# Expert choice with its token norms taken by VectorE from the transposed rows, and the expert weights loaded between those rows

## The chip, the cores and the metric

The kernel runs on one core of a Trainium2 chip. A core has a matrix engine (TensorE, in the profile PE, with its weight loads as PEld), a vector engine (VectorE, DVE), an engine for activations and copies (ScalarE, ACT), a general one (GpSimd, POOL) and SyncE (SP), which here only issues DMAs. Operands lie in SBUF (128 partitions), TensorE writes to PSUM (eight banks of 128 x 512 float32), and sixteen DMA engines carry data between SBUF and DRAM. The metric is the time of one execution in microseconds on the device; less is better.

## The reference

The program is a four-layer network on an image of 4 x 128 x 64 x 64 in float32: 4 batches of 4096 tokens of 128 channels. Each layer is a token mixer and a feed-forward part, both with residuals. The feed-forward part of layers 1 and 2 is a mixture of 64 experts in which each expert chooses its 8 tokens in each batch. The norm ahead of it has no weights. Cut to this part:

```python
def _ln_t(v, eps=1e-5):                       # per token, over 128 channels
    m = jnp.mean(v, axis=-1, keepdims=True)
    s = jnp.var(v, axis=-1, keepdims=True)
    return (v - m) / jnp.sqrt(s + eps)

def _L1_ffn_ref(x, gate_w, gate_b, weight1, weight2):
    logits = jnp.einsum('bsd,ed->bse', x, gate_w) + gate_b
    probs = jax.nn.softmax(logits, axis=1)                     # over the 4096 tokens
    vals, idx = jax.lax.top_k(probs.transpose(0, 2, 1), K)     # 8 tokens of each expert
    topv, topi = vals.transpose(0, 2, 1), idx.transpose(0, 2, 1)
    flat_idx = topi.reshape(Bn, K * E)
    gathered = jnp.take_along_axis(x, flat_idx[:, :, None], axis=1).reshape(Bn, K, E, Dn)
    pooled = jnp.einsum('bked,bke->bed', gathered, topv)
    ...                       # h = gelu([pooled, 1] @ weight1), out = [h, 1] @ weight2
    weighted = jnp.einsum('beo,bke->bkeo', out, topv).reshape(Bn, K * E, O)
    return jnp.zeros((Bn, Sn, O)).at[jnp.arange(Bn)[:, None], flat_idx].add(weighted)

t = t + _L1_ffn_ref(_ln_t(t), ...)            # layer 1; the same in layer 2
```

The logits of a token can be had from the token as it is: with a gate matrix from which the channel mean has been taken (`cent` @ gate), they are the product times 1/sqrt(variance + eps), plus the bias. Likewise the pooled token is `cent` times the sum of raw tokens, each weighted by its share times its 1/sqrt.

## The kernel before, in words

The activations `net.xs` stay in SBUF, channels on the partitions, tokens along the free axis; `net.chunk(b, c)` is chunk c (512 tokens, eight a batch) of batch b. `expert_choice` (L1246) is called for layers 1 and 2. Batches are worked on in two pairs, batches 0 and 1 and batches 2 and 3: the 64 experts of one batch lie on partitions 0 to 63, those of the other on 64 to 127.

Each call has three stages. Stage A finds norms, logits, choices and pooled tokens. Stage B is the experts' network, 16 groups of four experts (`first`, `turn`, `second`, `hand`), each group with two weight DMAs of 1 MiB (`load`, L1320 and L1322). Four groups have buffers of their own (`moe_w`) and are loaded ahead; the fifth buffer (`moe_w_b`) takes the place of stage A's pools, so its first load waits until those are released. Stage C adds the experts' outputs to the chosen tokens (L1629, L1633).

Stage A before, by its functions:

- `load` of four groups (8 MiB) comes first in the program.
- `stat(p, j)`: centres 512 tokens with a matmul by `cent` (L1343) and squares them on ScalarE (L1345). `variances` sums four squares over the channels with matmuls by `ewin` (L1353), so that one PSUM bank gathers the variances of a pair, 512 tokens to a partition. `scales` takes the square root on ScalarE (L1366), `inverted` the reciprocal on VectorE (L1370, 128 x 512). `turn_scales` transposes the scales so that tokens lie on partitions (L1376, L1378).
- `logits(p, c)`: a matmul broadcasts a chunk's scales to the experts' partitions (L1387), two gate matmuls make the raw logits (L1389), ScalarE copies the broadcast (L1393), VectorE multiplies (L1394), ScalarE adds the bias (L1395). The result stays in `chosen[p]`, 128 x 4096.
- `rows(b, c)`: four transposes put 512 tokens on partitions (L1417), ScalarE copies them into one of five buffers `xts` (L1419) with their scale behind them (L1420), and a DMA writes them to a table in DRAM, 144 floats a token (L1422).
- `largest(p)`: VectorE finds the 8 largest of 4096 logits in each partition and their places (L1428, L1431) and turns the places into table rows (L1433 to L1437). `exponentials` and `denominators` make the softmax sums on ScalarE (L1445, L1449). `ask(p, j)` gathers rows on POOL's queue (L1455).
- `pool(p)`: for each of the 8 choices VectorE makes a diagonal of share times scale (L1469) and TensorE adds up rows times diagonal (L1477); a copy, the matmul by `cent` (L1481) and the copy to `pooled` (L1482) follow.

TensorE, ScalarE, VectorE and POOL execute in the order in which the program is written (`manual_schedule(engines=ORDERED)`); a buffer taken from a pool makes an instruction wait until the previous user is done. SP's order is made by the framework's scheduler; SP executes its DMA issues one after another, so one that waits for data holds those behind it. The attention phase, which the prediction draws on, also has a scale row that goes to DRAM and is broadcast back (`att_spread`, L1922, and `att_by`, L1927), a root taken on VectorE in 14 steps (L1855 to L1861); and the last feed-forward part takes token statistics on VectorE (L2485).

Of the kernel before, what the change touches and what calls it, by code (L numbers as in the profile page):

```python
# [17 lines left out]
F32 = mybir.dt.float32  # L18
# [1227 lines left out]
def expert_choice(net, layer):  # L1246
# [20 lines left out]
    K, ROW = 8, P + 16  # L1267
# [3 lines left out]
    with ExitStack() as ctx:  # L1271
        dram = ctx.enter_context(tc.tile_pool(name="moe_dram", bufs=1, space=bass.MemoryType.DRAM))
        tables = [dram.tile([2 * N, ROW], F32, name=f"moe_table{p}") for p in range(PAIRS)]
# [24 lines left out]
        behind = keep.tile([P, 1], F32, name="moe_behind")  # L1298
        nc.gpsimd.memset(behind[0:E], 0.0)
        nc.gpsimd.memset(behind[E:P], float(N))  # L1300
# [24 lines left out]
        weights = [load(g) for g in range(EARLY)]  # L1325
        with (
# [5 lines left out]
            def bank(tag, name):  # L1332
                return ps.tile([P, CH], F32, name=f"moe_{name}", tag=tag, bufs={"a": 3, "b": 3}.get(tag, 1))

            stats = {}

            def stat(p, j):

                if j == 0:
                    stats[p] = (bank("pv", "pv"), [])  # L1340
                pv, squares = stats[p]
                pd = bank("a", "pd")
                nc.tensor.matmul(pd, net.cent, net.chunk(2 * p + j // NCH, j % NCH), start=True, stop=True)  # L1343
                sq = sb.tile([P, CH], F32, name="moe_sq", tag="moe_sq", bufs=5)
                nc.scalar.activation(sq, pd, AF.Square)  # L1345
                squares.append(sq)
                if j % 4 == 1 and j > 4:
                    variances(p, j // 4 - 1)

            def variances(p, r):  # L1350
                pv, squares = stats[p]
                for q in range(4):
                    nc.tensor.matmul(  # L1353
                        pv[32 * q : 32 * q + 32],
                        net.ewin[:, 31 - r : 63 - r],
                        squares[4 * r + q],
                        start=r == 0,
                        stop=r == 3,
                    )

            rstds, turned = {}, {}

            def scales(p):
                variances(p, 3)
                rstd = sb.tile([P, CH], F32, name="moe_rstd", tag="moe_rstd")
                nc.scalar.activation(rstd, stats[p][0], AF.Sqrt, bias=net.eps[1e-5])  # L1366
                rstds[p] = rstd

            def inverted(p):
                nc.vector.reciprocal(rstds[p], rstds[p])  # L1370

            def turn_scales(p):

                pt = bank("a", "pr")
                for k in range(4):
                    nc.tensor.transpose(pt[:, k * P : (k + 1) * P], rstds[p][:, k * P : (k + 1) * P], net.ident)  # L1376
                turned[p] = sb.tile([P, 2, NCH, 4], F32, name="moe_turned", tag="moe_turned")
                nc.vector.tensor_copy(  # L1378
                    turned[p].rearrange("p i (a q) k -> p k q (i a)", q=4),
                    pt.rearrange("p (k q r) -> p k q r", q=4, r=32)[:, :, :, 0:4],  # L1380
                )

            def logits(p, c):
                pb, pl = bank("b", "rb"), bank("a", "pl")
                q = c % 4
                rows = slice(32 * q, 32 * q + 32)
                nc.tensor.matmul(pb, own[rows, c // 4, :], rstds[p][rows], start=True, stop=True)  # L1387
                for i in range(2):
                    nc.tensor.matmul(  # L1389
                        pl[i * E : (i + 1) * E], cgate, net.chunk(2 * p + i, c), start=True, stop=True  # L1390
                    )
                lg = chosen[p][:, c * CH : (c + 1) * CH]
                nc.scalar.copy(lg, pb)  # L1393
                nc.vector.tensor_mul(lg, lg, pl)  # L1394
                nc.scalar.activation(lg, lg, AF.Identity, bias=gbias)  # L1395

            xts = [sb.tile([P, 4, ROW], F32, name=f"moe_xt{i}", bufs=1) for i in range(5)]
            for t in xts:
                nc.gpsimd.memset(t[:, :, P:ROW], 0.0)

            own = sb.tile([P, 2, 2 * E], F32, name="moe_own", bufs=1)
            for q in range(4):
                group = slice(32 * q, 32 * q + 32)
                for r in range(2):
                    for i in range(2):
                        at = 32 * q + 2 * i + r
                        nc.gpsimd.tensor_copy(
                            own[group, r, i * E : (i + 1) * E], net.ident[group, at : at + 1].to_broadcast([32, E])
                        )

            def rows(b, c):

                p, i = divmod(b, 2)
                pt = bank("b", "pt")
                for t in range(4):
                    tok = slice((4 * c + t) * P, (4 * c + t + 1) * P)
                    nc.tensor.transpose(pt[:, t * P : (t + 1) * P], net.xs[:, b, tok], net.ident)  # L1417
                xt = xts[(b * NCH + c) % len(xts)]
                nc.scalar.copy(xt[:, :, 0:P], pt.rearrange("p (t d) -> p t d", d=P))  # L1419
                nc.scalar.copy(xt[:, :, P], turned[p][:, i, c, :])  # L1420
                first = i * N + c * CH
                nc.sync.dma_start(tables[p][first : first + CH, :].rearrange("(t p) r -> p t r", p=P), xt)  # L1422

            places, shares, asked = {}, {}, {}

            def largest(p):
                top = keep.tile([P, K], F32, name=f"moe_top{p}")
                nc.vector.max(out=top, in_=chosen[p])  # L1428
                tops[p] = top
                place = sb.tile([P, K], U32, name="moe_place", tag="moe_place")  # L1430
                nc.vector.max_index(out=place, in_max=top, in_values=chosen[p])  # L1431
                row = sb.tile([P, K], F32, name="moe_row", tag="moe_row")
                nc.vector.tensor_copy(row, place)  # L1433
                nc.vector.tensor_scalar(row, row, behind, None, op0=ALU.add)
                places[p] = sb.tile([P, K], I32, name="moe_idx", tag="moe_idx")
                nc.vector.tensor_copy(places[p], row)
                nc.vector.tensor_scalar_mul(negs[p], top[:, 0:1], -1.0)  # L1437
# [3 lines left out]
            def exponentials(p, c):  # L1441

                sq = sb.tile([P, CH], F32, name="moe_sq", tag="moe_sq", bufs=5)
# [8 lines left out]
            def ask(p, j):  # L1452
                if j == 0:
                    asked[p] = sb.tile([P, K, ROW], F32, name="moe_asked", tag="moe_asked")
# [6 lines left out]

            def pool(p):

                nc.vector.reciprocal(totals[p], totals[p])
                nc.vector.tensor_scalar_mul(shares[p], shares[p], totals[p])
                acc = bank("acc", "acc")[:, 0 : 2 * E]
# [1185 lines left out]
```

## Time and profile before

| what | us |
|---|---|
| median of the runs (3) | 6021.36 (6016.81 to 6021.89) |
| the profiled execution's own time | 6020.81 |
| its span, first to last instruction | 6018.7 |
| stage A of layer 1 | 2466.5 to 2588.0, 121.5 |
| stage B of layer 1 | 2588.0 to 2665.0, 77.0 |
| stage A of layer 2 | 2933.7 to 3053.2, 119.5 |
| stage B of layer 2 | 3053.2 to 3130.0, 76.8 |
| mean granted TensorE clock | 0.975 of full speed |

The two stages A are 241 us, 4% of the span. Their end is taken where SP issues the first late weight load. Window rows are read thus: stretch in us, its length, then for each engine busy time and (instructions), the granted TensorE clock, the mean busy share of the DMA engines (the records can overlap, so a little over 1 is possible) and GB/s. Timeline rows: start, duration, engine, line, operation, output <- inputs, shapes, how many; in square brackets the idle time of the engine before it and what ended it. For SP (`SPq`) the duration is that of the issue, not of the transfer. Rows of waits: engine and line, what was waited for, us in total, times, the longest.

### The profile page before, as it was taken

How to read it: one execution, taken by the hardware profiler on the slowest of the kernel's cores; microseconds unless marked ns; L12 is line 12 of the kernel's file. 1: busy time of each engine (PE TensorE's matmuls, PEld its weight loads, DVE VectorE, ACT ScalarE, POOL GpSimd, SP SyncE). 2: the span in 40 equal slices, each digit the busy share in tenths (PEclk: the TensorE clock that was granted, in tenths of full speed). 3: DMA queues.
4: the chain of work that ended last, by engine and by line, in shares of the span. 5: the costliest groups of instructions: out<-in, count | busy, mean ns of one | idle time of the engine just before them, and what ended most of it. 6: DMA issues, size and time to landing. Idle time of an engine off the chain costs nothing. (4 is left out here: it accounts for less than half of the span.)

```text
span 6018.7 us, 97982 instructions
## 1 busy us (share of the span) xinstructions
PE 5660.1 (94%) x39902; PEld 2247.3 (37%) x39933; DVE 4413.8 (73%) x4945; ACT 3332.5 (55%) x4150; POOL 2057.3 (34%) x2015
## 2 busy tenths in 40 slices
PE   8999999889999988879979999999999999999699
PEld 2222222346677666433333222322232223222243
DVE  6888887456667676357446888888888888888687
ACT  4444444332333232431336888888888888899410
POOL 3898897027777777200010111111111111111100
PEclk9999999999999999989989999999999999999899
DMA  6434432047777777550274676656665666666300
GB/s 216 99 73 92 86 78 47 1 142 222 220 231 216 231 220 211 163 203 0 81 266 112 131 158 146 140 127 151 146 144 125 150 146 144 130 136 133 69 25 28
DMA packets 273275, 818.40 MB, mean 136 GB/s; under 512 B 42644, under 2 KB 100392, under 8 KB 226728
## 3 DMA queue, kind: packets, MB, share of 16 engines
q0 software_dynamic: 109568, 505.75, 35.4%
q1 hardware_dynamic: 163240, 306.20, 17.6%
q8 instruction: 320, 5.24, 0.4%
q14 instruction: 147, 1.20, 0.1%
HBM read 416.71 MB, written 93.13 MB: 85 GB/s over the span
## 5 line engine op out<-in xcount | busy, mean ns | idle before, releaser
L2035 ACT ACTIVATE att_ex<-att_sc,att_shift 128x1024 f32<-128x1024 f32 x2048 | 2141.7, 1111 | 282.6 <-PE att_sc L2031 167.7
L2066 DVE TENSOR_TENSOR att_dve<-att_dve,att_ex 128x2048 f32<-128x2048 f32 x704 | 1631.5, 2317 | 155.3 <-ACT att_ex L2035 130.5
L2031 PE MATMUL att_sc<-att_q,att_k 32*128 32x512 f32 x8192 | 1280.9, 640 | 0.5 <-ACT att_ex L2035 0.5
L2047 PE MATMUL att_pv<-att_ex,att_vals 128*32 128x512 f32 x8192 | 1091.9, 605 | 0.0
L998 POOL DMA_INDIRECT dcn_g<-dcn_table,dcn_idx x896 | 851.4, 950 | 354.2 <-issue 151.1
L412 DVE SCALAR_TENSOR_TENSOR inv_prod<-inv_pk,bspan,inv_seen 128x512 f32<-128x512 f32 (+1 forms) x1120 | 774.6, 743 | 140.1 <-PE inv_pk L399 139.8
L410 POOL TENSOR_TENSOR inv_prod<-inv_seen,inv_prod 128x512 f32<-128x512 f32 (+1 forms) x672 | 837.5, 1273 | 94.0 <-ACT inv_prod L409 94.0
L2064 POOL DMA_DIRECT2D att_dma<-att_ex x224 | 192.5, 860 | 1965.4 <-ACT att_ex L2035 1727.4
L409 ACT ACTIVATE inv_prod<-inv_pk,bspan 128x512 f32<-128x512 f32 (+1 forms) x672 | 436.1, 682 | 503.7 <-PE inv_pk L399 493.9
L2031 PEld LDWEIGHTS att_sc<-att_q,att_k 32*128 32x128 f32 x8192 | 423.0, 183 | 658.4 <-issue 417.1
L1006 DVE TENSOR_TENSOR dcn_g<-dcn_g,dcn_near_w 128x1024 f32<-128x1024 f32 x448 | 539.0, 1214 | 167.9 <-DMA dcn_g<-dcn_table,dcn_idx 151.7
L399 PE MATMUL inv_pk<-inv_red,wtap 32*96 32x512 f32 (+1 forms) x3584 | 511.4, 636 | 7.3 <-DVE wtap L377 7.3
L1015 PE MATMUL dcn_pt<-ident,dcn_g 128*128 128x128 f32 x3584 | 473.1, 276 | 37.5 <-ACT dcn_st L1120 12.6
L1015 PEld LDWEIGHTS dcn_pt<-ident,dcn_g 128*128 128x128 f32 x3584 | 418.9, 142 | 210.1 <-issue 122.7
L421 PE MATMUL inv_out<-inv_prod,inv_fold 96*32 96x512 f32 (+1 forms) x3584 | 477.9, 605 | 8.5 <-DVE xs L429 8.5
L2047 PEld LDWEIGHTS att_pv<-att_ex,att_vals 128*32 128x32 f32 x8192 | 161.2, 108 | 752.6 <-issue 727.4
L399 PEld LDWEIGHTS inv_pk<-inv_red,wtap 32*96 32x96 f32 (+1 forms) x3584 | 131.5, 170 | 385.6 <-DVE inv_prod L412 362.1
L1120 ACT COPY dcn_st<-dcn_pt 128x512 f32<-128x512 f32 x224 | 129.9, 580 | 241.2 <-PE dcn_pt L1015 241.2
L1034 ACT ACTIVATE dcn_fold<-dcn_pf,dcn_turn 128x256 f32<-128x256 f32 x128 | 60.2, 473 | 365.1 <-PE dcn_pf L1030 365.1
L1127 PE MATMUL dcn_out<-dcn_st,dcn_wk 128*128 128x512 f32 x448 | 237.4, 612 | 23.3 <-DVE xs L1135 21.4
L2554 PE MATMUL top_po<-top_xg,top_cwe 128*128 128x512 f32 x512 | 233.7, 597 | 0.0
L1054 DVE TENSOR_TENSOR dcn_square<-dcn_hx,dcn_by 128x512 f32<-128x512 f32 x192 | 130.1, 678 | 114.2 <-PE dcn_by L1040 75.2
(449 smaller groups left out, 5326.1 us busy)
## 6 DMA issues: line engine op xcount, KB each, us to landing
att_dma<-att_ex POOLq DMA_DIRECT2D x224, 1024.0 KB, 7.0
inv_seen<-inv_image SPq DMA_DIRECT2D x256, 266.0 KB, 9.1
moe_w<-in_L_ffn_weight SPq DMA_DIRECT2D x64, 1024.0 KB, 14.4
att_dma<-att_ex SPq DMA_DIRECT2D x32, 1024.0 KB, 11.2
att_dve<-att_dma POOLq DMA_DIRECT2D x32, 1024.0 KB
moe_table<-moe_xt SPq DMA_DIRECT2D x64, 288.0 KB, 2.8
dcn_table<-dcn_xt SPq DMA_DIRECT2D x32, 512.0 KB, 4.8
dcn_g<-dcn_table,dcn_idx POOLq DMA_INDIRECT x896, 3.7
```

Of the source, the lines that this page charges most:

```text
L399: nc.tensor.matmul(pk[0:m], wtap[half][rg, i, blk], red[rg, h * CH : (h + 1) * CH], start=True, stop=True)
L409: nc.scalar.activation(prod[0:m, h], pk[0:m], AF.Identity, bias=by)
L410: nc.gpsimd.tensor_mul(of, view, of)
L412: nc.vector.scalar_tensor_tensor(out=of, in0=as_shape(pk[0:m], of), scalar=by, in1=view, op0=ALU.add, op1=ALU.mult)
L421: nc.tensor.matmul(po[CR * blk : CR * (blk + 1), h, :], fold[0:m], prod[0:m, h, :], start=unit == 0, stop=unit == UNITS - 1,)
L998: nc.gpsimd.indirect_dma_start(out=g[:, t, :], out_offset=None, in_=rows, in_offset=bass.IndirectOffsetOnAxis(ap=idx[:, Q4 * c + i + t, k ...
L1006: nc.vector.tensor_mul(near, near, by)
L1015: nc.tensor.matmul(pt[0][:, (i + t) * P : (i + t + 1) * P], near[:, t, q, :], net.ident, is_transpose=True, start=i + t + q == 0, stop=i + ...
L2031: nc.tensor.matmul(pes[h // 2][:, h % 2, :], ks[r, t * P : (t + 1) * P], q[r], start=True, stop=True)
L2035: nc.scalar.activation(ex[:, 2 * two : 2 * two + 2, :], pes[two], AF.Exp, bias=shifts[g][:, two : two + 1],)
L2047: nc.tensor.matmul(block["pv"][r], vals[:, t, r], ex[:, h, :], start=t == 0, stop=t == NT - 1)
L2066: nc.vector.tensor_add(block[who], block[who], ex)
```

## The change

- Statistics: `rows(b, c)` now also makes them. The four transposes take every fourth token of a chunk (so that each partition holds four neighbouring tokens and the table is written in runs of 2 KB), and VectorE's `bn_stats` reads each 128 x 128 block from PSUM. `stat`, the `ewin` matmuls and `turn_scales` go. The table has 128 floats a token, without the scale.
- Scales: `scales(p)` makes variances (`variance`, five small steps), root, reciprocal (now 128 x 64) and one transpose; a row of scales goes to DRAM (`spread`) and comes back broadcast to the experts' partitions, chunk by chunk (`way`, two DMAs of 128 KB, three buffers `moe_by`), in place of the broadcast matmul.
- Logits: the multiply reads the broadcast and the product in the strided order in which the rows lie.
- Choice: `largest_of` finds the 8 largest of each chunk as it comes; `largest` finds the 8 largest among the 64 candidates and their table rows, with tables `behind` and `order` filled by POOL one column at a time.
- Pooling: the scale of the gathered rows is computed from the gathered rows themselves (`bn_stats`, `variance`, `inverse_root`) ahead of the diagonals.
- Order: rows of batches 0 and 1 first; the weight loads stand behind every second row of batch 1 instead of at the start; then the scales of pair 0, the centring of the gate, six rows of batch 2, and the logits of pair 0 with the remaining rows and the scales of pair 1 between them; the second pair's logits go along with the first pair's gathers and exponentials.

In the built program's order on SP, layer 2's loads stand behind 10, 12, 14 and 16 row writes; in layer 1 the first load stays ahead of the rows and the other three stand behind 12, 14 and 16. In both, the first `spread` row and the broadcasts `way` stand behind the last load.

```diff
-    K, ROW = 8, P + 16
+    K, HALVES = 8, 6
...
-        tables = [dram.tile([2 * N, ROW], F32, name=f"moe_table{p}") for p in range(PAIRS)]
+        tables = [dram.tile([2 * N, P], F32, name=f"moe_table{p}") for p in range(PAIRS)]
+        spread = [dram.tile([2, NCH, CH], F32, name=f"moe_spread{p}") for p in range(PAIRS)]
...
+        behind = keep.tile([P, NCH, K], F32, name="moe_behind")
+        for c in range(NCH):
+            nc.gpsimd.memset(behind[0:E, c, :], float(c * CH))
+            nc.gpsimd.memset(behind[E:P, c, :], float(N + c * CH))
+        order = keep.tile([P, NCH * K], F32, name="moe_order")
+        for i in range(NCH * K):
+            nc.gpsimd.memset(order[:, i : i + 1], float(i))
...
-        weights = [load(g) for g in range(EARLY)]
+        weights = []
...
+            def variance(halves, out, apart):
+                nc.vector.tensor_sub(apart, halves[..., 1], halves[..., 4])
+                nc.vector.tensor_mul(apart, apart, apart)
+                nc.vector.tensor_add(out, halves[..., 2], halves[..., 5])
+                nc.vector.scalar_tensor_tensor(
+                    out=out, in0=apart, scalar=P / 4.0, in1=out, op0=ALU.mult, op1=ALU.add
+                )
+                nc.vector.tensor_scalar(out, out, 1.0 / P, 1e-5, op0=ALU.mult, op1=ALU.add)
...
             def rows(b, c):
...
+                    nc.tensor.transpose(pt[:, t * P : (t + 1) * P], net.chunk(b, c)[:, t:CH:4], net.ident)
                 xt = xts[(b * NCH + c) % len(xts)]
+                nc.scalar.copy(xt, pt.rearrange("p (t d) -> p t d", d=P))
+                for t in range(4):
+                    nc.vector.bn_stats(halves[p][:, i, c, t, :], pt[:, t * P : (t + 1) * P])
                 first = i * N + c * CH
+                nc.sync.dma_start(tables[p][first : first + CH, :].rearrange("(p t) r -> p t r", t=4), xt)
...
             def scales(p):
...
+                variance(halves[p].rearrange("p i c t h -> p (i c t) h"), var, apart)
+                nc.scalar.activation(var, var, AF.Sqrt)
+                nc.vector.reciprocal(var, var)
                 pt = bank("a", "pr")
+                nc.tensor.transpose(pt[0 : 2 * NCH * 4, 0:P], var, net.ident)
+                lines = sb.tile([2 * NCH * 4, P], F32, name="moe_lines", tag="moe_lines", bufs=1)
+                nc.vector.tensor_copy(lines, pt[0 : 2 * NCH * 4, 0:P])
+                nc.sync.dma_start(spread[p].rearrange("i c (t q) -> (i c t) q", q=P), lines)
+                for c in range(2):
+                    way(p, c)
+
+            def way(p, c):
+                by = ways[p, c] = sb.tile([P, CH], F32, name="moe_by", tag="moe_by", bufs=3)
+                for i in range(2):
+                    nc.sync.dma_start(by[i * E : (i + 1) * E], spread[p][i, c : c + 1, :].to_broadcast([E, CH]))
...
             def logits(p, c):
-                pb, pl = bank("b", "rb"), bank("a", "pl")
...
-                nc.scalar.copy(lg, pb)
-                nc.vector.tensor_mul(lg, lg, pl)
+                by = ways.pop((p, c)).rearrange("p (t q) -> p q t", t=4)
+                nc.vector.tensor_mul(lg.rearrange("p (q t) -> p q t", t=4), by, pl.rearrange("p (q t) -> p q t", t=4))
                 nc.scalar.activation(lg, lg, AF.Identity, bias=gbias)
+                if c + 2 < NCH:
+                    way(p, c + 2)
...
+            def largest_of(p, c):
+                lg = chosen[p][:, c * CH : (c + 1) * CH]
+                nc.vector.max(out=peaks[p][:, c, :], in_=lg)
+                nc.vector.max_index(out=spots[p][:, c, :], in_max=peaks[p][:, c, :], in_values=lg)
...
             def largest(p):
...
+                nc.vector.max(out=top, in_=flat)
+                nc.vector.tensor_scalar_mul(negs[p], top[:, 0:1], -1.0)
+                nc.vector.max_index(out=place, in_max=top, in_values=flat)
+                nc.vector.tensor_copy(at, place)
+                nc.vector.tensor_copy(known, spots[p])
+                nc.vector.tensor_add(known, known, behind)
+                for j in range(K):
+                    nc.vector.scalar_tensor_tensor(
+                        out=found[:, j, :],
+                        in0=order,
+                        scalar=at[:, j : j + 1],
+                        in1=known.rearrange("p c k -> p (c k)"),
+                        op0=ALU.is_equal,
+                        op1=ALU.mult,
+                    )
...
             def pool(p):
...
+                for j in range(K):
+                    nc.vector.bn_stats(own[:, j, :], asked[p][:, j, :])
+                var, root, spare = (small[:, n] for n in range(3))
+                variance(own, var, spare)
+                inverse_root(root, var, spare, small[:, 3].bitcast(I32))
+                nc.vector.tensor_mul(shares[p], shares[p], root)
                 for j in range(K):
...
+                    nc.vector.tensor_scalar(diag, net.ident, shares[p][:, j : j + 1], None, op0=ALU.mult)
+                    nc.tensor.matmul(acc, asked[p][:, j, :], diag, start=j == 0, stop=j == K - 1)
...
+            for b in range(2):
+                for c in range(NCH):
+                    rows(b, c)
+                    if b and c % 2:
+                        weights.append(load(len(weights)))
             scales(0)
...
+            left = [(b, c) for b in range(2, B) for c in range(NCH)]
+            for _ in range(6):
+                rows(*left.pop(0))
             for c in range(NCH):
                 logits(0, c)
+                for _ in range(2):
+                    if left:
+                        rows(*left.pop(0))
+                        if not left:
+                            scales(1)
+                if c > 0:
+                    largest_of(0, c - 1)
+            largest_of(0, NCH - 1)
             largest(0)
             for c in range(NCH):
                 logits(1, c)
+                ask(0, c)
+                exponentials(0, c)
+                if c > 0:
+                    largest_of(1, c - 1)
             denominators(0)
+            largest_of(1, NCH - 1)
             largest(1)
+            for c in range(K):
+                ask(1, c)
                 exponentials(1, c)
             denominators(1)
             pool(0)
...
             pool(1)
```

## The prediction

> **What bounds the kernel now.** I read the page's first part for the balance of engines, then the table of windows for the two passes through `expert_choice`, then the issue queue of SP (SyncE) and its waits for the moment that ends the changed part, and last the timeline of VectorE for prices. TensorE leads overall, but the diff touches only stage A of each pass (statistics, logits, choice, gather, pooling), so the window table counts:
>
> ```profile
> PE 5660.1 (94%) x39902; PEld 2247.3 (37%) x39933; DVE 4413.8 (73%) x4945; ACT 3332.5 (55%) x4150; POOL 2057.3 (34%) x2015
> ```
> ```profile
> core 0: us, PE busy (x) PEld busy (x) DVE busy (x) ACT busy (x) POOL busy (x), PEclk, DMA share, GB/s
> 2466.50:2588.00 121.50, 102.89 (x402) 44.96 (x402) 44.03 (x59) 73.70 (x168) 16.24 (x23) 0.91 0.48 151
> 2588.00:2665.00 77.00, 59.50 (x768) 33.53 (x768) 27.67 (x47) 26.75 (x39) 0.00 (x0) 0.89 0.90 328
> 2933.70:3053.20 119.50, 101.07 (x402) 44.43 (x402) 44.16 (x60) 72.31 (x167) 19.15 (x42) 0.91 0.52 162
> 2940.00:2960.00 20.00, 20.00 (x70) 7.16 (x66) 3.75 (x3) 10.82 (x18) 0.00 (x0) 1.00 1.05 383
> ```
>
> Rows one and three are stage A of layers 1 and 2: 121.5 and 119.5 us, bound by TensorE (103 and 101 us busy), with VectorE at 44. Row two is the experts' stage behind it, fed by DMA at 328 GB/s; the diff leaves it alone. The last row is a stretch in which only the first weights move: 383 GB/s, so 1 MiB takes 2.74 us.
>
> The issue queue of SP, layer 2 (the last two lines are from the attention phase), and SP's waits there:
>
> ```profile
> 2936.55 0.59 SPq L1320 DMA_DIRECT2D moe_w<-in_L_ffn_weight  x1
> ...
> 2946.98 2.58 SPq L1322 DMA_DIRECT2D moe_w<-in_L_ffn_weight  x1
> ...
> 3178.73 0.34 SPq L1922 DMA_DIRECT2D att_spread<-att_scale  x1
> 3180.20 0.81 SPq L1927 DMA_DIRECT2D att_by<-att_spread  x2
> ```
> ```profile
> 4671.51 0.33 SPq L1922 DMA_DIRECT2D att_spread<-att_scale  x1
> 4676.55 0.81 SPq L1927 DMA_DIRECT2D att_by<-att_spread  x2
> ```
> ```profile
> SPq L1320 <- DMA moe_asked<-moe_table,moe_idx: 15.8, 1, 15.8
> SPq L1320 <- PE moe_pc L1481: 1.4, 1, 1.4
> ```
>
> The first weights past the preload wait for the gathered rows and for the last product of stage A (`moe_pc`). Those late weights use addresses of stage A's pools in the changed kernel too, so the DMA-bound stage starts when stage A ends, and the change is worth what it does to stage A's length, twice. Also: a scale row written to DRAM lets its readers issue 1.47 us later on an idle queue, 5.04 us later on a busy one.
>
> VectorE's prices:
>
> ```profile
> 2960.33 0.69 DVE L1394 TENSOR_TENSOR moe_chosen<-moe_chosen,moe_pl 128x512 f32<-128x512 f32 x1 [1.92 <-PE moe_pl L1389]
> 2976.23 4.43 DVE L1428 MAX8 moe_top<-moe_chosen 128x8 f32<-128x4096 f32 x1 [0.79 <-ACT moe_chosen L1395]
> ...
> 2980.77 4.42 DVE L1431 FIND_INDEX8 moe_place<-moe_top,moe_chosen 128x8 uint32<-128x4096 f32 x1
> ```
> ```profile
> 5669.77 3.32 DVE L2485 BATCH_NORM_STATS2 top_halves<-top_pd 128x6 f32<-128x128 f32 x16
> ```
> ```profile
> 3183.43 0.69 DVE L1938 TENSOR_TENSOR att_k<-att_by,att_sc 128x512 f32<-128x512 f32 x1 [4.76 <-DMA att_by<-att_spread]
> ```
>
> **The change part by part.** Removed per layer, mostly from TensorE's 101 us: 32 centring matmuls (two passes of about 0.43 us each, 27 us), 32 variance and 16 broadcast matmuls; from ScalarE 32 squares (0.60) and 16 copies (0.58); from VectorE two reciprocals of 3.35 and two searches of 4.43 + 4.42. That takes TensorE to some 40 us and ScalarE to some 45: neither bounds any more. VectorE gains 128 token-block statistics (3.32/16 = 0.21 us each, 26.6 us), 16 more of gathered rows, 16 searches over 512 and, for each pair, some 40 small dependent steps. It becomes the bound, and the order of work decides how well it is fed. I walk along that order, from stage A's start.
>
> (a) *First weights.* They no longer start at once but behind the first of batch 1's pairs of row writes: in layer 2 behind ten row writes (about 8.5 us at some 0.8 us a row: 4 statistics); in layer 1 one load stays early and the rest follow twelve rows (about 11.5). To the first bytes I add 1.4, as for the scale row above.
>
> (b) *Drain.* In SP's issue order the scale row (`moe_spread`) stands behind four loads and six row writes of 256 KB in layer 2 (9.5 MiB), three loads and four rows in layer 1 (7 MiB). The old loads show SP blocked (the last held it 2.58 us), so the queue is full. 9.5 x 2.74 = 26.0 and 7 x 2.74 = 19.2: reached at 35.9 and 32.1 us. The scales themselves are ready at about 18.
>
> (c) *Scale row out, broadcast back.* From its issue at 3178.73 to the multiply at 3183.43 the same pair takes 4.7 us. First logits at 40.6 in layer 2 (before: 2960.33 - 2933.7 = 26.6) and 36.8 in layer 1 (before 29.8). VectorE has only 22 rows x 0.83 = 18 us to do meanwhile: it idles about 15.
>
> On this place the Trainium skill has a rule that speaks against the change: "DMA: Bandwidth & Descriptors", section "Queues, rings and completion order", says that on each DMA engine descriptors are consumed in ring order, so a small transfer issued behind megabytes waits for them. The two scale rows above (1.47 and 5.04 us) agree in direction, but neither stands behind this much. By the rule the full drain counts, as in (b). If only the busy row's delay counted, first logits would come 4.7 + 3.6 after the scales at 18, at 26, and both layers would be some 10 to 15 us shorter.
>
> (d) *From first logits to the end.* No row shows a search over 512. In proportion to the 4096-wide rows (1.08 ns an element) one costs 0.55; at the rate of the multiply of 512 (0.69, 1.35 ns) 0.70. I take the second, the row of that size: twice 0.70 and the value load 0.09, 1.5 per chunk. The lower end would give 16 x 0.3 = 5 us a layer back. Pair 0: chunk 0 2.5; chunks 1 to 3 multiply 0.69, eight statistics 1.66, search 1.52, in all 3.95 each; chunk 4 the same and the second pair's scale chain (3.15); chunks 5 to 7 2.25 each; a stall of 1.7 for the last broadcast, which SP sends behind the second scale row; the last search 1.5. Sum 31.4. Choice among 64 candidates: 16 small steps at 0.21, 3.4. Pair 1: 8 x 2.25, and 2.0 for a reduction and waits for its first broadcasts, 20. Tail: ScalarE's eight exponentials at 0.70 and the sum, 6.4 (the gathers, 8 x 1.25 on POOL, run beside them and land in pool(0)'s shadow); pool(0): two small steps 0.4, eight statistics 1.7, variance 5 x 0.21, the 14-step root (3.07 in the attention phase, 3174.76 to 3177.83), a multiply, then diagonals to pooled 5.1 (3041.29 to 3046.33), `b1t` 0.7: 12.3; pool(1) 11.7. Sum 31.4 + 3.4 + 20 + 30.4 = 85.2.
>
> Before, pooling a pair took 5.6 to 6.2, so the second statistics of the gathered rows alone put some 12 us on the end path. The rest of (d) gains against the old 93 (2960.33 to 3053.2).
>
> (e) *Costed at nothing.* 80 one-column fills on POOL (0.14 apart, 11 us): their first reader comes 70 us in; uncovered, 11. Row writes of 2 KB runs instead of 576 B: landing, now 2.8 us, hides behind five buffers. `moe_by` broadcasts, 32 of 128 KB: two chunks ahead of use while their landing stays under 2 x 2.25. The gate's centring, moved behind the scales: 0.5 us of TensorE, which waits for DMA then; uncovered, 0.5. TensorE at a lower clock: once idle 2.59 us it took 2.06 us for eight transposes (0.26 each), against 3.16 for twenty (0.16). At twice the usual times two rows and two gate matmuls come to 4.0 us, level with VectorE's 3.95, so I take nothing; if they go one after the other instead of side by side, 1 us for each of 5 chunks, 10 over both layers:
>
> ```profile
> 3025.24 3.16 PE L1417 MATMUL moe_pt<-ident,xs 128*128 128x128 f32 x20 [1.29 <-ACT moe_xt L1419]
> 3030.99 2.06 PE L1417 MATMUL moe_pt<-ident,xs 128*128 128x128 f32 x8 [2.59 <-ACT moe_xt L1419]
> ```
>
>
> Sum: layer 2 40.6 + 85.2 = 125.8 against 119.5, +6.3; layer 1 36.8 + 85.2 = 122.0 against 121.5, +0.5. The profiled execution took 6020.8 (span 6018.7 and 2.1 around it), 0.6 under the median of 6021.4: 6020.8 + 6.8 = 6027.6, so 6028. About 0.2% (12 us) is what a measurement of this kernel can tell from no change.
>
> **The rivals.** *Broadcasts land late* (slower): for attention's 256 KB broadcasts issue to landing is 6.2 us at the median, 3.6 at best. If `moe_by` takes the longer, pair 1's eight chunks, 2.25 each with three buffers, wait: about 9 us a layer, 18 in all, 6046. It decides from 0.7 us over my landing; against it, half the bytes and a free queue by then.
>
> *VectorE dearer* (slower): the multiply reads the broadcast and PSUM at a stride of four, which no row shows for this form. From the plain row up to double: 16 x 0.69 x 2 = 22 us, 6050; less than plain I exclude, as the elements are the same.
>
> *The scale row does not queue* (faster): first logits at 22.4, when rows and scales are done; 18 and 14 saved, and with the waits of (d) unchanged the sum falls to about 5995. For it speaks that `moe_table` rows land in 2.8 us at the median; but those are issued after the weights have drained. Against it, the busy scale row's 5.04 and SP's blocked issues.
>
> *The loads do not move* I exclude: SP's order in the built program has them between the rows, but for layer 1's first.
>
> **How the numbers follow.** Forecast 0.47 (own range 6005 to 6040, from cheaper searches, 5 a layer, and half the queue on one side, the slower clock on the other: within 0.2% 0.29, slower 0.13, faster 0.05); late broadcasts 0.20 (slower 0.18, same 0.02); dearer VectorE 0.15 (0.13, 0.02); no queue 0.18 (faster 0.16, same 0.02). Together faster 0.21, same 0.35, slower 0.44. The range reaches from the no-queue case's middle to just over the dearer VectorE's: 5995 to 6052.
>
> **What would show it.** Right: stage A at 122 to 126 us; VectorE 85 to 100 us busy in it, TensorE under 45; a gap of some 15 us on VectorE ahead of the first logits, ended by a broadcast whose scale row was written long after its issue; gathered rows' statistics and root, 6 us, twice at the end. Wrong: first logits near 22 us (no queue); VectorE waiting for `moe_by` in pair 1 (late broadcasts); L1394's successor over 1 us (stride); and, outside the cases, an experts' stage other than 77 us.

## The result, and the profile after

The changed kernel takes 6053.06 us at the median of four runs (6049.69 to 6056.97), the kernel before 6021.62; the ratio is 1.005 with a 95% interval from 1.0039 to 1.0062. It is slower, by about 31 us; 6028 was forecast, with a range up to 6052. The direction was the likelier one, the size between four and five times too small (6.8 us forecast).

To see where the time came from, one length is used throughout: from the last write of tokens in the phase ahead to the copy of pair 1's pooled tokens (L1482 before, L1492 after). It is read off VectorE's timeline.

| us | layer 1, first logits | layer 1, end | layer 2, first logits | layer 2, end |
|---|---|---|---|---|
| before | 37.8 | 129.6 | 27.4 | 120.2 |
| changed | 49.6 | 141.6 | 44.4 | 136.7 |

The two stages A are longer by 12.0 and 16.5 us, 28.5 in all. The profiled execution (6056.97) is 36.2 over the one of before (6020.81) and 4 over its own median; stage B stayed at 80.0 and 78.2 us from the pooled copy to the first scatter (78.3 and 78.2 before). What else separates the two executions lies in phases that the change doesn't touch.

The page's first part, the windows of the two stages of the changed kernel, and those of layer 2 cut at the first logits, at the end of pair 0's search, and at the end of pair 1's:

```profile
PE 5585.6 (92%) x39570; PEld 2234.9 (37%) x39601; DVE 4505.3 (74%) x5467; ACT 3273.8 (54%) x3992; POOL 2057.8 (34%) x2129
```
```profile
2455.80:2597.40 141.60, 60.18 (x237) 36.79 (x237) 91.78 (x325) 44.61 (x89) 19.87 (x101) 0.64 0.48 159
...
2947.20:3083.90 136.70, 59.13 (x236) 34.36 (x236) 90.97 (x322) 43.12 (x88) 19.87 (x101) 0.65 0.49 164
2947.20:2991.60 44.40, 23.71 (x119) 17.42 (x119) 20.72 (x97) 13.06 (x24) 4.70 (x85) 0.76 0.90 321
2991.60:3030.70 39.10, 18.49 (x61) 7.12 (x57) 28.92 (x79) 10.82 (x19) 0.00 (x0) 0.63 0.44 147
3030.70:3054.20 23.50, 7.54 (x20) 1.53 (x20) 22.18 (x51) 12.78 (x26) 7.58 (x8) 0.65 0.32 79
3054.20:3083.90 29.70, 9.38 (x40) 8.30 (x40) 19.15 (x98) 6.47 (x19) 7.59 (x8) 0.52 0.07 18
```

TensorE's work in layer 2 fell from 101 to 59 us of the stage and VectorE's rose from 44 to 91, so the bound moved as forecast. But VectorE is busy in only two thirds of the stage, and in its first 44 us (third row) less than half, while the DMA engines run at 90%. What SP issues in the second half of that stretch, and what VectorE waits for in the whole stage (engine, line and what was waited for: us in total, times, the longest):

```profile
2969.26 2.92 SPq L1364 DMA_DIRECT2D moe_table<-moe_xt  x2
2972.22 0.63 SPq L1325 DMA_DIRECT2D moe_w<-in_L_ffn_weight  x1
2973.84 2.11 SPq L1327 DMA_DIRECT2D moe_w<-in_L_ffn_weight  x1
2976.05 2.44 SPq L1378 DMA_DIRECT2D moe_spread<-moe_lines  x1
2978.59 2.23 SPq L1364 DMA_DIRECT2D moe_table<-moe_xt  x3
2987.23 2.38 SPq L1385 DMA_DIRECT2D moe_by<-moe_spread  x4
```
```profile
DVE moe_halves L1362 <- ACT moe_xt L1360: 26.8, 12, 6.4
DVE moe_chosen L1395 <- DMA moe_by<-moe_spread: 4.5, 2, 2.3
```

The scale row, 32 KB, holds SP for 2.44 us at its issue, and its readers go out 8.74 us after that (2978.49 to 2987.23). In the kernel before, on an idle queue, 1.13 us passed between the end of such an issue and the readers' (3179.07 to 3180.20 in attention). The largest wait is not the broadcast, though: the statistics wait 26.8 us in layer 2 for the row copies on ScalarE. Of this 6.3 us is the wait shown further below; for most of the rest the copies in turn wait for buffers, which the row writes have not yet freed:

```profile
ACT moe_xt L1360 <- DMA moe_table<-moe_xt: 21.1, 7, 7.3
```

The two waits end close together. The last of the six rows of batch 2 is done at 2989.4, and the first multiply then waits 2.16 us more for its broadcast:

```profile
2988.54 0.89 DVE L1362 BATCH_NORM_STATS2 moe_halves<-moe_pt 128x6 f32<-128x128 f32 x4 [5.03 <-ACT moe_xt L1360]
2991.59 1.04 DVE L1395 TENSOR_TENSOR moe_chosen<-moe_by,moe_pl 128x512 f32<-128x512 f32 x1 [2.16 <-DMA moe_by<-moe_spread]
```

VectorE's timeline shows the other new sight, one step of pair 0 (multiply, two rows' statistics, the search of the chunk before):

```profile
2995.49 1.04 DVE L1395 TENSOR_TENSOR moe_chosen<-moe_by,moe_pl 128x512 f32<-128x512 f32 x1
2997.80 1.68 DVE L1362 BATCH_NORM_STATS2 moe_halves<-moe_pt 128x6 f32<-128x128 f32 x8 [1.26 <-ACT moe_xt L1360]
2999.40 0.67 DVE L1406 MAX8 moe_peaks<-moe_chosen 128x8 f32<-128x512 f32 x1
3000.11 0.09 DVE L1407 MATCH_VALUE_LOAD moe_spots<-moe_peaks,moe_chosen 128x8 f32 x1
3000.18 0.69 DVE L1407 FIND_INDEX8 moe_spots<-moe_peaks,moe_chosen 128x8 uint32<-128x512 f32 x1
3000.79 1.03 DVE L1395 TENSOR_TENSOR moe_chosen<-moe_by,moe_pl 128x512 f32<-128x512 f32 x1
```

From multiply to multiply it is 5.3 us, not 3.95: the multiply costs 1.04 where 0.69 was taken, and the statistics stand idle 1.26 us in each of the five steps that have rows. ScalarE's lines of the same step show what they wait for, the bias addition and then the copy of the first row:

```profile
2996.57 0.72 ACT L1396 ACTIVATE moe_chosen<-moe_chosen,moe_gbias 128x512 f32<-128x512 f32 x1 [2.23 <-DVE moe_chosen L1395]
2997.20 1.05 ACT L1360 COPY moe_xt<-moe_pt 128x512 f32<-128x512 f32 x2
```

One thing about the multiply's strides: as the kernel is written, `lg.rearrange("p (q t) -> p q t")` and the same view of the product step through neighbouring elements. Only the broadcast is read out of order, four values that lie 128 floats apart and then the next four.

### The profile page after: what moved, and what is told of

Its sections match the earlier page's. It is cut to its first block, busy times and chain, and to the rows that moved or that the text cites. A ratio compares the mean times of both kernels' runs of the same rounds, so it can differ in the third digit from the quotient of the medians.

```text
span 6055.1 us, 97860 instructions
## 1 busy us (share of the span) xinstructions
PE 5585.6 (92%) x39570; PEld 2234.9 (37%) x39601; DVE 4505.3 (74%) x5467; ACT 3273.8 (54%) x3992; POOL 2057.8 (34%) x2129
## 3 DMA queue, kind: packets, MB, share of 16 engines
q1 hardware_dynamic: 144104, 312.63, 17.6%
q14 instruction: 153, 1.25, 0.1%
## 5 line engine op out<-in xcount | busy, mean ns | idle before, releaser
L1120 ACT COPY dcn_st<-dcn_pt 128x512 f32<-128x512 f32 x224 | 129.9, 580 | 243.0 <-PE dcn_pt L1015 243.0
```

## The experiments

The theory to be tested: stage A is longer because (1) rows, scale row and broadcasts queue behind the weights, 12 us (layer 1) and 17 us (layer 2) of delay to the first logits; (2) the statistics wait for ScalarE, where the bias addition stands ahead of the row copies; (3) the strides of the multiply cost 0.35 us each; (4) the gathered rows' second statistics lie on the path. Rivals are named in each expectation.

The chips of these runs take some 200 us longer for the kernel before as well (in the gathers of layer 1's deformable phase, untouched), so only stage lengths are compared, and ratios to the kernel before on the same chip. Where no ratio is given, the kernel was executed once. The changed kernel was run on one of these chips too.

**The changed kernel on one of those chips.**

> The changed kernel as it is, beside the kernel before on the same chip as the other runs. Theory: its cost lies in stage A and does not depend on the chip: stages of 141 and 137 us (before 129.6 and 120.2), 28 us in all, ratio 1.0045. Rival: on this chip, where the untouched deformable phase takes 200 us longer, the change costs something else: a ratio outside 1.002 to 1.007.

Measured: ratio 1.0034 (1.0020 to 1.0048), stages of 141.0 and 135.6 us. The cost is where it was: 26.8 us over the two stages of the kernel before as first traced, and 26.8 of 6234 is 0.43%, inside the interval. Against the first trace of the same kernel the stages differ by 0.6 and 1.1 us, so differences of about 1 us in the stage lengths below say nothing.

**The weights issued late.** They go behind pair 1's last broadcast, and SP keeps the written order in stage A, so that the scheduler doesn't pull them ahead:

```diff
-            tc.manual_schedule(engines=ORDERED),
+            tc.manual_schedule(engines=ORDERED | {ENG.SP}),
...
                     rows(b, c)
-                    if b and c % 2:
-                        weights.append(load(len(weights)))
...
                 if c > 0:
                     largest_of(1, c - 1)
+                if c == NCH - 3:
+                    weights.extend(load(g) for g in range(EARLY))
```

> Only the place of the first four groups' weight loads differs from the changed kernel: they are issued behind the last broadcast of pair 1 (SP follows the written order in stage A), some 35 us before the stage's end. Lengths are counted from the last token write of the phase before to the copy of pair 1's pooled tokens; the changed kernel has 141.6 us in layer 1 and 136.7 in layer 2, the one before 129.6 and 120.2. Theory 'queue': row writes, scale row and broadcasts wait behind the loads. First logits then come at about 33 us in layer 1 (now 49.6) and 24 in layer 2 (now 44.4), the stages shrink to about 125 and 117, and the time is about 6053 - 36 = 6017. Rival 'no queue': the scale row is slow by itself, first logits stay within 3 us, time 6048 to 6056. Rival 'paid later': first logits come early, but the gathers or the experts' stage wait for the late loads and give back 10 us or more a layer, 6035 or more.

Measured: first logits at 37.0 and 27.7 us, stages 129.0 and 119.7, ratio to the kernel before 0.9991 (0.9980 to 1.0003). Stage B begins its scatter 79.7 and 78.3 us after the pooled copy, so nothing is paid later: the weights' 8 MiB still have 38 us. SP's queue:

```profile
3170.41 0.47 SPq L1378 DMA_DIRECT2D moe_spread<-moe_lines  x1
3172.21 2.38 SPq L1385 DMA_DIRECT2D moe_by<-moe_spread  x4
...
3233.18 0.59 SPq L1325 DMA_DIRECT2D moe_w<-in_L_ffn_weight  x1
```

The readers now issue 1.33 us after the scale row's issue, and the row buffers no longer hold ScalarE: the scales are copied out 18.3 us into layer 2 instead of 24.9. The place of the loads makes the whole difference to the kernel before. (SP's written order came with this edit, and its own part was not measured.) From first logits to the end the stages take 92.0 us, as in the changed kernel (92.0 and 92.3): the delay was pure shift. The first logits themselves came 4 us later than expected in both layers: the six rows of batch 2 stand ahead of them on VectorE, and the last of these still waits 2.46 us for its copy.

**The weights first, as in the kernel before.**

```diff
-        weights = []
+        weights = [load(g) for g in range(EARLY)]
...
-                    if b and c % 2:
-                        weights.append(load(len(weights)))
```

> The loads stand ahead of all rows, as in the kernel before; the rest is the changed kernel. Theory 'queue': the first row writes now wait behind up to 8 MiB (22 us), the five row buffers fill and the rows stall instead of the scale row. In layer 2 first logits stay at 40 to 46 us (now 44.4), the stage at 133 to 139, and the time lies within 10 us of 6053. Rival 'the place between the rows does the harm': with the weights out of the way early, first logits come at about 30 in layer 2, time about 6053 - 26 = 6027.

Measured: first logits at 53.2 and 48.0, stages 145.2 and 140.2, ratio 1.0049 (1.0034 to 1.0064). Both a little over the expected bounds, and on the theory's side. VectorE's timeline shows the rows stopping as soon as five buffers are full:

```profile
3170.37 4.05 DVE L1362 BATCH_NORM_STATS2 moe_halves<-moe_pt 128x6 f32<-128x128 f32 x20 [1.58 <-ACT moe_xt L1360]
3197.78 8.81 DVE L1362 BATCH_NORM_STATS2 moe_halves<-moe_pt 128x6 f32<-128x128 f32 x44 [23.36 <-ACT moe_xt L1360]
```

A wait of 23.4 us after 20 blocks (five rows), close to 8 x 2.74 = 21.9 us for the weights. The kernel before could load first because it wrote no row until its first logits were done.

**Two groups between the rows, two late.**

```diff
-                    if b and c % 2:
+                    if b and c % 4 == 3:
...
+                if c == NCH - 3:
+                    weights.extend(load(g) for g in range(2, EARLY))
```

SP is in written order here too.

> Two of the four groups' weights stay between the rows of batch 1, two go behind the last broadcast. Theory 'queue': the delay is the bytes ahead of the scale row, so 4 MiB less are 11 us less: first logits at 31 to 36 us in layer 2 (44.4 with four groups, 27.7 with none), the stage at 123 to 128. Rival 'it is a threshold' (the delay comes when SP or the row buffers block at all): first logits within 3 us of 44 or of 28.

Measured: first logits in layer 2 at 37.3 us, the stage 129.8: 1.3 and 1.8 us over the expected bounds, but 7.1 and 9.6 us from the two ends. In layer 1, which had no forecast, they come at 46.0, between 37.0 with none and 49.6 with four groups. So the delay grows with the bytes and doesn't jump at a threshold; that it is in proportion to them isn't shown. In this run VectorE's last wait ahead of the first logits of layer 2 is one of 10.08 us for a row of batch 2: in the written order SP issues those rows only behind the broadcasts, which wait for the scale row.

**Another queue for the scales.** The scale row and its broadcasts are issued by GpSimd (`nc.gpsimd.dma_start` in `scales` and `way`); loads and rows stay on SP.

> The scale row and its broadcasts go through GpSimd's queue instead of SP's; loads and row writes stay. Theory A, the scale row's place in the queue is what holds the first logits: they come about 6 us behind the ready scales (29.6 and 24.9), so at 36 and 31 us, and the stages lose 13 us each. Theory B, the row buffers hold them: six rows of batch 2 stand ahead of the logits on VectorE and their buffers wait for row writes that stay behind the loads (the last of the six ends at about 42 in layer 2): first logits at 42 to 44, and the stages lose 3 us at most.

Measured: first logits at 51.3 and 47.0, stages 143.2 and 140.2: no gain, 1.6 and 3.5 us more than the changed kernel. That is theory B's side, though 5 us over its 42 to 44 in layer 2. The broadcasts went out at 30.7 us in layer 2, but VectorE was at a row:

```profile
3205.29 1.68 DVE L1362 BATCH_NORM_STATS2 moe_halves<-moe_pt 128x6 f32<-128x128 f32 x8 [4.95 <-ACT moe_xt L1360]
3216.76 0.89 DVE L1362 BATCH_NORM_STATS2 moe_halves<-moe_pt 128x6 f32<-128x128 f32 x4 [9.79 <-ACT moe_xt L1360]
3217.57 1.03 DVE L1395 TENSOR_TENSOR moe_chosen<-moe_by,moe_pl 128x512 f32<-128x512 f32 x1
```

The multiply starts with no wait for its broadcast, right after the last of the six rows of batch 2, which had waited 9.79 us. So two chains go behind the weights, and either alone can hold the first logits: the scale row, which ended last in the changed kernel, and the row writes that free the five buffers, which end last here. The prediction had only the first.

**The bias behind the rows.** The addition leaves `logits` and becomes a function of its own:

```diff
                 logits(0, c)
                 for _ in range(2):
                     if left:
                         rows(*left.pop(0))
                         if not left:
                             scales(1)
+                biased(0, c)
                 if c > 0:
                     largest_of(0, c - 1)
```

> On ScalarE the bias addition of a chunk is written behind the copies of the two rows of the same step instead of ahead of them. Theory: in the changed kernel the statistics wait 1.26 us in each of five steps of pair 0 for a row copy that stands behind the bias addition, which waits for the multiply; the step goes from 5.28 us to 4.0 to 4.3, the stage loses 5 to 6.5 us in each layer, and the time is about 6053 - 12 = 6041. Rival: TensorE at its lower clock feeds the rows no faster than 5 us a step, and the stage stays within 2 us.

Measured: stages 134.6 and 129.9, 7.0 and 6.8 us shorter than in the first trace of the changed kernel, a little over the 5 to 6.5 expected; ratio 1.0026 (1.0017 to 1.0036). The wait is gone, and the step is 3.9 us:

```profile
3204.44 1.04 DVE L1395 TENSOR_TENSOR moe_chosen<-moe_by,moe_pl 128x512 f32<-128x512 f32 x1
3205.41 1.67 DVE L1362 BATCH_NORM_STATS2 moe_halves<-moe_pt 128x6 f32<-128x128 f32 x8
...
3208.38 1.04 DVE L1395 TENSOR_TENSOR moe_chosen<-moe_by,moe_pl 128x512 f32<-128x512 f32 x1
```

In the changed kernel the chain of one step was multiply, bias on ScalarE (0.72), first row copy (0.58), statistics. The trace names ScalarE's copy as what released the statistics in all five steps. By their data the statistics need TensorE's transposes only, but they are written behind the copy of the same PSUM tile. (The other order of those two was not tried.)

**A multiply without strides.**

```diff
-                by = ways.pop((p, c)).rearrange("p (t q) -> p q t", t=4)
-                nc.vector.tensor_mul(lg.rearrange("p (q t) -> p q t", t=4), by, pl.rearrange("p (q t) -> p q t", t=4))
+                nc.vector.tensor_mul(lg, ways.pop((p, c)), pl)
```

> The multiply of the logits takes its operands and writes its result without strides, so logits are scaled by the wrong tokens' scales; nothing else differs. Theory: VectorE paces both logit loops, one multiply goes from 1.04 to 0.69 us, and the stages lose 16 x 0.35 = 5.6 us each (136.0 and 131.1). Rival: the time goes into waits for ScalarE and the broadcasts, 2 us or less each.

Measured: 136.6 and 131.4, that is 5.0 and 5.3 us less (5.6 expected), with multiplies of 0.67 to 0.69 us. The strided read is paid almost in full.

**No second statistics.** `bn_stats`, `variance` and `inverse_root` leave `pool`.

> The statistics, variance and root of the gathered rows are left out, so the pooled tokens lack their norm's scale. Theory 'all on the path': two chains of 6.0 us lie between choice and pooled tokens, the stages lose 12 us each (129.6 and 124.7). Rival 'gathers next': without them pair 1's pooling waits for its gathers (issued in 10 us after the choice, landed some 13 behind it), and the stages lose 7 to 8 us each.

Measured: 131.4 and 125.9, 10.2 and 10.8 us less. Nearer to 12 than to 7.5: nearly all of it is on the path. VectorE waits for no gather in this run; in layer 2 the two chains turn out as 5.7 and 5.5 us, and 1.1 us of what is freed goes to longer waits for TensorE.

**All together.** The late weights, the bias behind the rows, a gate matmul that reads its tokens in the scales' order (so that the multiply is plain, and the bias addition reads its input across the strides; the expectation says that it writes them), and the statistics taken apart from the pooling:

```diff
+                        pl[i * E : (i + 1) * E].rearrange("p (t q) -> p t q", t=4),
+                        cgate,
+                        net.chunk(2 * p + i, c).rearrange("p (q t) -> p t q", t=4),
...
+                nc.vector.tensor_mul(by, by, pl)
...
+                nc.scalar.activation(lg.rearrange("p (q t) -> p q t", t=4), by, AF.Identity, bias=gbias)
...
+            statistics(0)
             denominators(1)
+            diagonals(0)
...                                   # transposed biases b1t
+            statistics(1)
+            finish(0)
+            diagonals(1)
+            finish(1)
```

> Four edits of the changed kernel in one, all in stage A: the weights behind the last broadcast (as in loads_late, which had stages of 129.0 and 119.7 us); the bias addition behind the row copies (as in bias_behind_rows, 7 us less a layer); the gate matmul reads its tokens in the order of the broadcast scales, so that VectorE's multiply has no strides and the bias addition writes the strided result; and the statistics of the gathered rows are taken apart from the pooling, pair 0's while ScalarE finishes pair 1's exponentials, pair 1's while TensorE ends pair 0's pooling. Theory 'VectorE is the bound and the terms add': 7 for the bias, 16 x 0.35 = 5.6 for the multiply, about 3.5 for the statistics; stages of 113 and 104 us, 16 us under the kernel before in each layer, time 0.5% under it. Rival 'something else bounds by then' (TensorE's lower clock in pair 0's steps, the row buffers, the gathers, which end only 13 us behind the choice): stages of 119 and 110 or more, at most 0.35% under it.

Measured: stages 120.4 and 111.7, ratio 0.9964 (0.9950 to 0.9978). Faster than both kernels, but of the 16 us of terms only half came: the rival holds. VectorE now waits elsewhere:

```profile
3200.53 0.69 DVE L1398 TENSOR_TENSOR moe_by<-moe_by,moe_pl 128x512 f32<-128x512 f32 x1 [3.46 <-DMA moe_by<-moe_spread]
...
3244.63 0.42 DVE L1558 COPY moe_b1t<-moe_pb 128x256 f32<-128x256 f32 x1 [4.26 <-PE moe_pb L1557]
```

**Those two waits taken out.** Pair 1's first broadcasts take their buffers after pair 0's last, and `b1t` is made behind the gate's centring:

```diff
-                for c in range(2):
-                    way(p, c)
+                if p == 0:
+                    for c in range(2):
+                        way(p, c)
...
                 if c + 2 < NCH:
                     way(p, c + 2)
+                elif p == 0:
+                    way(1, c + 2 - NCH)
```

> all_together (stages 120.4 and 111.7 us) with two more moves: pair 1's first broadcasts take their buffers behind pair 0's last one, which in all_together came so late that VectorE stood 3.5 us, and the transposed biases of the experts are made at the start instead of between the two poolings, where VectorE waited 4.3 us for them. Theory 'both waits go': 3 us for the broadcasts, and 2 of the 4.3, since pair 1's gathered rows land only 2 us earlier: stages of about 115.5 and 107, ratio about 0.995 to 0.9965. Rival: both only uncover the next wait, stages within 2 us of all_together's.

Measured: 117.6 and 107.4, ratio 0.9946 (0.9931 to 0.9961). It beats the kernel before by some 0.5%, with 12.0 and 12.8 us less in its two stages; these make 0.40%, just inside the interval. The two moves gave 2.8 and 4.3 us; layer 1 stays 2 us over its forecast. The window of layer 2:

```profile
3124.30:3231.70 107.40, 62.44 (x236) 32.18 (x236) 85.06 (x321) 51.19 (x88) 19.85 (x101) 0.77 0.62 209
```

VectorE is busy for 85 of 107 us. One of its waits left is for the last gathered rows (1.40 us).

## Why the prediction was right or wrong

*What bounds:* right. TensorE left the bound, VectorE took it at 91 us (85 to 100 forecast). TensorE's own time was missed: 59 us, not 40 to 45. The granted clock fell from 0.91 to 0.65 over the stage of layer 2, and the same instructions grew longer there: the mean transpose from 0.300 to 0.352 us, the mean gate matmul from 0.641 to 0.868. How much of the miss that is was not separated.

*Late weights enter when stage A ends, so the change is worth twice stage A:* right. 28.5 of the 31 us lie there.

The prediction counted stage A from 8.0 us after the last write in layer 1 and 0.7 in layer 2; its terms are set on that count here.

*(a) to (c), first logits at 36.8 and 40.6:* measured 41.6 and 43.7. The mechanism (bytes ahead in the queue) is shown by the weights issued late, first, and in part; the sizes were 4.8 and 3.1 short. SP's timeline gives the parts (layer 1, layer 2): the loads behind the rows go out at 14.3 and 9.5 us, not at (a)'s 11.5 and 8.5; from there to the readers' issue takes 0.9 and 1.0 us longer than (b)'s drain; and from that issue to the multiply it is 4.3 and 4.4 us, where the row behind (c) has 3.2.

Another step failed beside these, (b)'s "The scales themselves are ready at about 18". The rows write through the same queue and have five buffers, so the loads stall the rows too, and the scales were copied out at 24.2 in layer 2 on the prediction's count (17.6 without the loads). By SP's timeline that cost nothing by itself in this kernel, since SP came to the scale row only at 28.1. But it hides a second chain. The idea of part (e) that the row writes hide "behind five buffers" is the same slip. That moving the scale row to another queue brings the first logits no earlier shows that this second chain alone is about as long as the first.

*(d), 85.2 us from first logits to the end:* measured 92.0 and 92.3. The mis-sized term is pair 0's loop, 31.4 forecast against 39.1 (2991.59 to 3030.72). It missed the round trip of 1.26 us for which the statistics wait behind the bias addition, in each of five steps, 6.3 us: this wait was in no rival. Taken out, the rest was 85.3 and 85.4 us. That this is 85.2 is partly luck: the multiplies' strided read (5 us, the second rival's mechanism at half its price, 1.04 instead of up to 1.38) is in it, and smaller misses elsewhere paid for it. The prediction has that stride at four floats on the broadcast and on PSUM; in the kernel it is 128 floats, on the broadcast alone. The second pair's scale chain was about as priced. Pair 1's loop took 23.5 with its predecessor's choice, as forecast (20 + 3.4), with dearer multiplies and fewer waits; the tail 29.7 (30.4 forecast). The searches over 512 cost 0.67, 0.09 and 0.69, as taken.

*(d)'s "the second statistics of the gathered rows alone put some 12 us on the end path":* right in kind, 10.2 and 10.8 when left out.

*(e):* the broadcasts land in 3.5 us at the median, so the rival *Broadcasts land late* is out; what VectorE waits for them after the first logits, 2.3 us, comes from one broadcast that SP sends behind the second scale row, for which (d) had 1.7. The fills on POOL cost nothing. The slower clock of TensorE did not pace the steps: with the bias moved they take 3.9 us at a granted clock of 0.71 in pair 0's loop (0.63 in the changed kernel).

*The scale row does not queue:* out. It took 8.7 us where the queue without the loads gave 1.3.

*The Trainium skill's rule:* "DMA: Bandwidth & Descriptors", section "Queues, rings and completion order", was weighed as speaking against the change. These runs agree with it for the scale row on SP's queue: 8.7 us behind the loads, 1.33 with none. They also show its reach: the rule is about the transfer that waits, and ahead of the first logits of layer 2 VectorE waited 16.4 us, in three waits, for rows whose buffers the waiting transfers held, against 2.2 for the broadcast itself.

The sum of the misses is 3.1 + 7.1 in layer 2 and 4.8 + 6.8 in layer 1, 21.8 us, against 28.5 - 6.8 = 21.7 measured. (The two agree by construction, as both are counted on the same lengths.) The time came out 1 us above the range's end, whose upper cases had no term for the round trip on ScalarE or for the rows' stall.

## What to carry to other kernels

A large prefetch put among small transfers on one queue delays everything whose completion frees a buffer there: ask for every transfer behind it both who reads it and what it releases. When an engine that was never the bound becomes it, read the written order of the *other* engines around its inputs: an addition that waits for it, written ahead of a copy that it waits for, is a round trip in each step. And an edit whose arithmetic is good can lose by its order alone: the same instructions, with the loads later, were level with the kernel before, and with four more moves (the bias, the strides, the statistics, two waits) 0.5% faster.

## What the runs showed of the hardware

- VectorE's multiply of 128 x 512 in which one operand is read in steps of 128 floats takes 1.00 to 1.05 us, without that 0.67 to 0.69. On ScalarE the bias addition of the same size takes 0.71 to 0.72 us plain and 1.16 to 1.25 when it reads its input in those steps.
- With TensorE busy for 59 of 137 us its granted clock was 0.65 in the stage and 0.52 in the tail, against 0.91 with 101 of 120 busy.
- The unit cost of the statistics held over two kernels: 0.207 us for a 128 x 128 block, 26.5 us for 128 of them, from PSUM and under load.
- Issued by GpSimd, the same small scale row let its readers go out 4.50 us after its issue, while the weights and rows on SP's queue were still moving, against 8.7 on SP's own.
